# One-hots, gathers and turns in the expert stage of a gated cross-attention kernel

## The chip, the cores and the metric

The kernel runs on one core of one Trainium2 chip. The metric is the device time of one execution in microseconds (us). Before the change three runs took 1636.4, 1639.86 and 1645.21 us; the median, 1639.86, is the time before. A core has five engines, each with a queue of its own that it works off strictly in order: TensorE (PE in the profile; its weight loads are shown apart as PEld), VectorE (DVE), ScalarE (ACT), GpSimd (POOL) and SyncE (SP). [...]POOL, SP and ACT also issue transfers (DMAs).

## The reference

`x` is 4 batches of 512 rows of 512 numbers. Four residual blocks follow each other, each on a layer norm of `x`, each scaled by a gate:

```python
x = x + jnp.tanh(g_xattn[0]) * _L0_xattn_ref(_layernorm(x, axis=-1), fside_BxS2xS2_0, ctx_1024)
x = x + jnp.tanh(g_ffn[0]) * _L0_ffn_ref(_layernorm(x, axis=-1), L0_ffn_w_fc, L0_ffn_w_proj)
x = x + jnp.tanh(g_xattn[1]) * _L1_xattn_ref(_layernorm(x, axis=-1), ctx_1024, mask_BxS2_bf1, L1_xattn_Wq, L1_xattn_Wk, L1_xattn_Wv, L1_xattn_Wo)
x = x + jnp.tanh(g_ffn[1]) * _L1_ffn_ref(_layernorm(x, axis=-1), L1_ffn_router_w, L1_ffn_norm_w, L1_ffn_gate_w, L1_ffn_up_w, L1_ffn_down_w)
```

The first is a pair of 8-bit quantized linears, the second a ternary feed-forward, the third attention with 16 heads. The change concerns the fourth, a mixture of 8 experts of which each row uses the best 2:

```python
logits = router_in @ router_w.T
probs = jax.nn.softmax(logits, axis=-1)
topw, topi = jax.lax.top_k(probs, TOP_K)
topw = topw / jnp.sum(topw, axis=-1, keepdims=True)
cw = jnp.zeros((T, E), flat.dtype).at[jnp.arange(T)[:, None], topi].add(topw)
g = jnp.einsum('td,edf->tef', flat, gate_w)
u = jnp.einsum('td,edf->tef', flat, up_w)
a = jax.nn.silu(g) * u
expert_out = jnp.einsum('tef,efd->ted', a, down_w)
y = jnp.einsum('ted,te->td', expert_out, cw) * SCALE
```

## The kernel before

The kernel doesn't compute every expert for every row. It sorts the 2048 x 2 pairs of row and expert by expert into at most 39 tiles of 128 pairs (`NSEG`), each tile of one expert, and runs only these. Tiles 0 to 15 (`NA`) are full tiles found among the first three batches while the attention of the fourth is still running; tiles 16 to 38 (`NB`, 23 of them) hold the rest, and are found when the fourth batch has been routed.

Routing (`route`, from L709) normalizes a batch, scores the experts on TensorE, ranks them on VectorE and writes the rows, with their 8 weights behind the 512 numbers, to a table in memory (`xtab`). Sorting (`sort`, from L845) gives each pair a place, and then inverts the map from pair to place: with `hi` (the tile) and `lo` (the row in the tile) of each pair it builds one-hots, `in_row` (128 x 128 for each of 24 or 32 groups of rows, L907) and `in_seg` (two per group, as wide as there are tiles, L909; the second of the two is made by GpSimd), and sums their products on TensorE (L914) into the list of row numbers of each tile, `ids` (L925; `aids` for the first part, `bids` for the second). Both are generators: `step_beside` runs them a step at a time between pieces of other work, up to the next `yield`.

For each tile j the expert stage then does:

- `fetch`/`gather` (L985): an indirect DMA from POOL's queue brings the 128 rows, 520 wide, into one of eight buffers `xg`.
- turn: the rows must lie across the partitions for the matmuls. Either TensorE transposes them (`prepare`, `turn_by_tensor`, L1098, and VectorE copies the result, L1099), for the tiles in `by_tensor` (0 to 3, 16 to 19, 36 to 38); or VectorE transposes 32 x 32 blocks (`turn_rows`, L520) and, once four tiles are done, 16 transfers from SP set the blocks in place (L1089).
- `hide` (L1107) and `expert_in` (L1000): the gate and up products (L1005), silu on ACT (L1006), and on VectorE the product with the up half and the row's weight (L1007). `weight_of` (L992) picks that weight, `cwj`, from the gathered row by two small VectorE instructions (L996, L997), called from `hide`.
- `turn_hidden` (L1113): TensorE transposes the 128 x 256 result, VectorE copies it (L1099).
- `expert_out` (L1120): the down product (L1124), a copy on ACT to one of three buffers `y` (L1128), and an indirect scatter-add from POOL's queue onto the output (L1129). Each scatter waits for the one before to land, because two of them may add to the same row.

The loop at the end (from L1155) runs j from 0 to 39: fetch up to 9 tiles ahead, turn up to 6 ahead, `hide(j)`, `prepare(j + 1)`, `turn_hidden(j - 1)`, `expert_out(j - 2)`, two steps beside. The first two tiles are gathered and run in the last steps of the attention loop (`start_tile`, L1015), which is otherwise a steady round of four groups of matmuls a head (L599, L612, L637, L651) with their weights loaded from POOL's queue (L578 to L593).

The order in which an engine meets its instructions isn't that of the program. A scheduler reorders each engine's instructions before the kernel is built, by when it believes their inputs to be ready and by their place in the program. An instruction may so be set ahead of another that is needed sooner; on the chip, everything behind it waits.

## Time and profile before

The profiled execution took 1645.29 us; its span, from the first to the last instruction, is 1643.3 us.

| What | Value |
|---|---|
| TensorE busy in the span | 1522.8 us (93%) |
| VectorE, ScalarE, GpSimd busy | 926.9, 566.6, 465.8 us |
| mean granted TensorE clock | 0.972 |
| attention ends, expert stage begins | about 1380 us |
| TensorE busy from 1430 to 1640 us | 185.44 of 210 us, clock 0.96 |
| VectorE busy from 1430 to 1640 us | 63.74 of 210 us |
| scatter-adds (L1129): first and last start | 1401.1 and 1637.4 us |
| scatter-add, from issue to landing | median 4.8 us (2.7 to 6.3) |
| gather (L989), from issue to landing | median 3.9 us (3.3 to 7.3) |

In the timelines a row is: start in us, length in us, engine, line, operation, output and inputs, shapes, how many instructions were merged into the row, and in brackets how long the engine stood idle before it and what ended that wait. `x8` on a tile's matmuls means eight records for four products in 32-bit numbers. The chain of waits is followed back from the last instruction; its shares are of the whole span.

### The profile page before, as it was taken

To read this page: it belongs to the slowest core of one execution; us is meant where nothing else is said; L and a number is where in the kernel's file an instruction comes from. 1 tells how busy PE (TensorE), PEld (TensorE's weight loads), DVE (VectorE), ACT (ScalarE), POOL (GpSimd) and SP (SyncE) were. 2 spreads that over 40 slices of the span, in tenths; PEclk is the share of its full clock that TensorE was granted. 3 is DMA by queue.
4 is the path that set the end of the run, shared out by engine and by line. 5 is a ranking of instruction groups with operands and counts; after the bars stand their busy time and mean duration, and the time that the engine had idled before them with its cause. 6 is when DMAs were issued, how large, how long until landed. Compare 5 with 4: busy or idle time off the path is not lost. (4 is left out here: it accounts for less than half of the span.)

```text
span 1643.3 us, 16405 instructions
## 1 busy us (share of the span) xinstructions
PE 1522.8 (93%) x4404; PEld 785.6 (48%) x4412; DVE 926.9 (56%) x2422; ACT 566.6 (34%) x1180; POOL 465.8 (28%) x605
## 2 busy tenths in 40 slices
PE   4777888999999999999999999999999998978997
PEld 2434555676434444445444445444454444644563
DVE  5666777672155555585665765565758555734221
ACT  2645453633233333353333442333523322211111
POOL 1254324342211113131131131131314112454333
PEclk9997999999999999999999998999999999889999
DMA  8551200113445455575454574464754655457532
GB/s 299 200 191 66 65 20 33 31 67 90 134 137 151 139 140 154 141 208 156 106 160 136 155 195 117 133 184 134 200 158 134 159 144 151 105 104 154 103 64 28
DMA packets 115146, 215.59 MB, mean 131 GB/s; under 512 B 29984, under 2 KB 34080, under 8 KB 115056
## 3 DMA queue, kind: packets, MB, share of 16 engines
q1 hardware_dynamic: 72336, 103.89, 22.2%
q0 software_dynamic: 30896, 88.57, 21.6%
q10 hardware_dynamic: 11824, 22.09, 4.0%
q8 instruction: 37, 0.61, 0.2%
q14 instruction: 53, 0.43, 0.1%
HBM read 98.76 MB, written 35.72 MB: 82 GB/s over the span
## 5 line engine op out<-in xcount | busy, mean ns | idle before, releaser
L617 DVE CUSTOM_DVE_ANT_0 e<-bank,mask_b 128x512 f32<-128x512 f32 x256 | 175.1, 689 | 258.7 <-PE bank L612 258.5
L612 PE MATMUL bank<-kT,qT 128*128 128x512 f32 x512 | 232.3, 593 | 0.7 <-ACT dn L458 0.7
L651 PE MATMUL acc<-wo,oT 128*128 128x512 f32 x512 | 232.5, 596 | 0.3 <-ACT oT L641 0.3
L637 PE MATMUL bank<-eT,v 128*128 128x512 f32 x512 | 230.4, 592 | 1.8 <-DVE nmax L617 1.8
L620 ACT ACTIVATE e<-e,nmax 128x512 f32<-128x512 f32 x256 | 184.3, 720 | 97.5 <-DVE nmax L617 90.8
L599 PE MATMUL bank<-gu,wq 128*128 128x512 f32 x384 | 178.0, 601 | 2.3 <-DVE nmax L617 2.3
L514 DVE STREAM_TRANSPOSE blocks<-e 128x512 f32<-128x512 f32 x256 | 158.9, 678 | 22.6 <-DMA eT<-blocks 17.9
L637 PEld LDWEIGHTS bank<-eT,v 128*128 128x128 f32 x512 | 97.2, 190 | 124.6 <-issue 110.7
L651 PEld LDWEIGHTS acc<-wo,oT 128*128 128x128 f32 x512 | 97.7, 191 | 123.2 <-issue 120.3
L612 PEld LDWEIGHTS bank<-kT,qT 128*128 128x128 f32 x512 | 96.9, 190 | 124.7 <-issue 114.3
L641 ACT COPY oT<-bank 128x512 f32<-128x512 f32 x64 | 37.5, 585 | 300.4 <-PE bank L637 279.9
L578 POOL DMA_DIRECT2D wq<-in_L_xattn_Wq_dram x64 | 48.5, 758 | 265.3 <-PE bank L599 245.1
L599 PEld LDWEIGHTS bank<-gu,wq 128*128 128x128 f32 x384 | 73.2, 192 | 93.7 <-issue 82.2
L593 POOL DMA_DIRECT2D wo<-in_L_xattn_Wo_dram x64 | 36.9, 577 | 255.5 <-PE acc L651 250.4
L628 DVE TENSOR_SCALAR e<-e,rt 128x512 f32<-128x512 f32 x256 | 107.7, 484 | 2.1
L1005 PE MATMUL acc<-gu,turned 128*128 x224 | 102.9, 602 | 0.0
L603 ACT ACTIVATE qT<-bank 128x512 f32<-128x512 f32 x64 | 38.2, 597 | 170.2 <-PE bank L599 164.5
L405 PE MATMUL acc<-pjT,hT 128*128 128x512 f32 x320 | 87.5, 403 | 5.7 <-DVE hT L430 5.7
L418 PE MATMUL bank<-xfT,fcT 128*128 128x512 f32 x320 | 88.2, 407 | 0.0
L1005 PEld LDWEIGHTS acc<-gu,turned 128*128 128x128 f32 x224 | 65.9, 295 | 33.5 <-issue 8.2
L1124 PE MATMUL acc<-dn,hidT 128*128 x156 | 77.1, 619 | 0.6 <-DVE hidT L1099 0.6
L429 POOL TENSOR_TENSOR r<-r 128x512 f32<-128x512 f32 x40 | 42.2, 1058 | 95.5 <-ACT hT L428 95.5
(339 smaller groups left out, 2045.2 us busy)
## 6 DMA issues: line engine op xcount, KB each, us to landing
eT<-blocks SPq DMA_DIRECT2D x1016, 64.0 KB, 2.8
wq<-in_L_xattn_Wq_dram POOLq DMA_DIRECT2D x64, 256.0 KB, 3.9
wo<-in_L_xattn_Wo_dram POOLq DMA_DIRECT2D x64, 256.0 KB, 3.3
kd<-dn SPq DMA_DIRECT2D x32, 256.0 KB, 2.4
vd<-dn SPq DMA_DIRECT2D x32, 256.0 KB, 2.0
kT<-kd POOLq DMA_DIRECT2D x32, 256.0 KB, 3.9
v<-vd POOLq DMA_DIRECT2D x32, 256.0 KB, 4.0
turned<-blocks SPq DMA_DIRECT2D x112, 64.0 KB, 3.1
```

The lines of the kernel that those rows point to most:

```text
L405: nc.tensor.matmul(outs[t], lhsT=h[:, t * P : (t + 1) * P], rhs=pjT[:, j, :], start=(j == 0 and u == 0), stop=(j == NH - 1 and u == 1),)
L418: nc.tensor.matmul(ps, lhsT=fcT[:, i, j * P : (j + 1) * P], rhs=xT[u][:, i, :], start=(u == 0 and i == 0), stop=(u == 1 and i == KD - 1),)
L514: nc.vector.transpose(blocks[:, :, :, t, :].rearrange("p c s r -> p s c r"), src.rearrange("p (s c i) -> p s c i", c=NQ, i=Q))
L599: nc.tensor.matmul(ps, lhsT=th[:, i, :], rhs=xT[:, :, i, :], start=(i == 0), stop=(i == KD - 1))
L612: nc.tensor.matmul(ps, lhsT=qT[:, t * P : (t + 1) * P], rhs=kT, start=True, stop=True)
L617: nc.vector.tensor_tensor_reduce(e, ps, mask_b[b], -1.0, 3.0e38, ALU.add, ALU.min, nmax[:, t : t + 1])
L620: nc.scalar.activation(e, e, AF.Exp, bias=nmax[:, t : t + 1], scale=-1.0, accum_out=total[:, t : t + 1])
L628: nc.vector.tensor_scalar(es[:, t, :], es[:, t, :], rt[:, t : t + 1], None, ALU.mult)
L637: nc.tensor.matmul(ps, lhsT=v[:, s, :], rhs=eT[:, :, s, :], start=(s == 0), stop=(s == NT - 1))
L651: nc.tensor.matmul(sums[b][t], lhsT=oT[:, t * P : (t + 1) * P], rhs=to, start=(n == 0), stop=(n == NHEAD - 1))
L1005: nc.tensor.matmul(ps, lhsT=xgT[k], rhs=gu[:, bass.ds(e, 1), k, :], start=(k == 0), stop=(k == KD - 1))
L1124: nc.tensor.matmul(ps, lhsT=hT[f], rhs=dn[:, bass.ds(e, 1), f, :], start=(f == 0), stop=(f == NF - 1))
```

## The change

Six things change.

1. One-hots: the 24 or 32 small pairs of instructions become a few wide ones on VectorE, with broadcast operands. GpSimd makes none of them any more. There are fewer `yield`s, so the row numbers are traced a step or so earlier.
2. The first matmul over the one-hots, every gather, and every turn on VectorE are kept in program order: `tc.keep_in_program_order` sets an instruction behind the one traced before it on the same engine (an order only, no wait for it to finish). Others may still move around it.
3. The weight of a row is read where the tile is turned (`weigh_rows`), into a column of a small tile that lives for the whole stage, not where the product needs it. The buffer of gathered rows is free from then on.
4. Tiles 4 to 7 join the tiles turned by TensorE.
5. The copy of rows turned by TensorE (in `prepare`) goes from VectorE to ScalarE.
6. Leads: a tile turned by TensorE is fetched 4 steps ahead, one turned by VectorE 10 ahead and turned 7 ahead.

```diff
     def turn_tile_apart(src, blocks, t):
-        nc.vector.transpose(
+        return nc.vector.transpose(
...
+    tile_base = cp.tile([P, TT], F32, name="tile_base")
...
+        nc.vector.tensor_scalar(tile_base, col[:, :TT], float(P), None, ALU.mult)
...
-        for i in range(TOPK * nt):
-            s, t = divmod(i, nt)
-            nc.vector.tensor_scalar(in_row[:, i, :], col, lo[:, s, t : t + 1], None, ALU.is_equal)
-            for u, v in enumerate((row1[:, 0:1], float(P * t))):
-                (nc.gpsimd if u else nc.vector).tensor_scalar(in_seg[:, i, u, :], cols, hi[:, s, t : t + 1], v, ALU.is_equal, ALU.mult)
-            if i % 4 == 3:
+        m = TOPK * nt
+        at_tile = hi.rearrange("p s t -> p (s t)").unsqueeze(2).to_broadcast([P, m, n])
+        at_row = lo.rearrange("p s t -> p (s t)").unsqueeze(2).to_broadcast([P, m, P])
+        nc.vector.tensor_tensor(in_seg[:, :, 0, :], cols.unsqueeze(1).to_broadcast([P, m, n]), at_tile, ALU.is_equal)
+        for s in range(TOPK):
+            mine = slice(s * nt, (s + 1) * nt)
+            nc.vector.tensor_tensor(
+                in_seg[:, mine, 1, :],
+                in_seg[:, mine, 0, :],
+                tile_base[:, :nt].unsqueeze(2).to_broadcast([P, nt, n]),
+                ALU.mult,
+            )
+        nc.vector.tensor_scalar(in_seg[:, :, 0, :], in_seg[:, :, 0, :], row1[:, 0:1], None, ALU.mult)
+        yield
+        for i in range(0, m, 4):
+            nc.vector.tensor_tensor(
+                in_row[:, i : i + 4, :],
+                col.unsqueeze(1).to_broadcast([P, 4, P]),
+                at_row[:, i : i + 4, :],
+                ALU.is_equal,
+            )
+            if i % 8 == 4:
                 yield
+        yield
         ps = work_tile()
         for i in range(TOPK * nt):
-            nc.tensor.matmul(
+            mm = nc.tensor.matmul(
...
+            if i == 0:
+                tc.keep_in_program_order(mm)
...
-        nc.gpsimd.indirect_dma_start(xg, None, table, bass.IndirectOffsetOnAxis(ap=ids, axis=0))
+        tc.keep_in_program_order(
+            nc.gpsimd.indirect_dma_start(xg, None, table, bass.IndirectOffsetOnAxis(ap=ids, axis=0))
+        )
         return xg, owned

-    def weight_of(xg, owned):
-        cwj = small(1, "cwj")
+    row_weight = cp.tile([P, NSEG], F32, name="row_weight")
+    def weigh_rows(j, xg, owned):
         junk = small(NE, "junk")
         nc.vector.tensor_tensor(junk, xg[:, D:], owned, ALU.mult)
-        nc.vector.tensor_reduce(cwj, junk, AX.X, ALU.add)
-        return cwj
+        nc.vector.tensor_reduce(row_weight[:, j : j + 1], junk, AX.X, ALU.add)
...
-        nc.vector.scalar_tensor_tensor(h, h, cwj, ps[:, FE:], ALU.mult, ALU.mult)
+        nc.vector.scalar_tensor_tensor(h, h, row_weight[:, j : j + 1], ps[:, FE:], ALU.mult, ALU.mult)
...
-    by_tensor = {j for j in range(NSEG) if j < NT or j // NT == NA // NT or j >= NSEG - NSEG % NT}
+    by_tensor = {j for j in range(NSEG) if j < 2 * NT or j // NT == NA // NT or j >= NSEG - NSEG % NT}
...
-        turn_tile_apart(
-            got[j][0][:, :D], blocks_of[g].rearrange("p c (s t r) -> p c s t r", s=KD, t=NT), t
+        xg, owned = got.pop(j)
+        tc.keep_in_program_order(
+            turn_tile_apart(xg[:, :D], blocks_of[g].rearrange("p c (s t r) -> p c s t r", s=KD, t=NT), t)
         )
+        weigh_rows(j, xg, owned)
...
-    def turn_by_tensor(src, n, dst):
+    def turn_by_tensor(src, n, dst, copy=nc.vector.tensor_copy):
...
-            turned_in[j] = turn_by_tensor(got[j][0], KD, dst)
+            turned_in[j] = turn_by_tensor(got[j][0], KD, dst, nc.scalar.copy)
+            weigh_rows(j, *got.pop(j))
...
-    GATHER, TURN = 9, 6
-    next_fetch, next_turn = len(first), NT
+    lead = {j: 4 if j in by_tensor else 10 for j in range(len(first), NSEG)}
+    TURN = 7
+    to_fetch = sorted(lead, key=lambda j: (max(j - lead[j], 0), j))
+    to_turn = [j for j in to_fetch if j not in by_tensor]
     for j in range(NSEG + 1):
         known = NSEG if len(found) == NSEG else NA
-        while next_fetch < min(j + GATHER, known):
-            fetch(next_fetch)
-            next_fetch += 1
-        while next_turn < min(j + TURN + 1, next_fetch):
-            turn_rows(next_turn)
-            next_turn += 1
+        for t in [t for t in to_fetch if t - lead[t] <= j and t < known]:
+            fetch(t)
+            to_fetch.remove(t)
+        while to_turn and to_turn[0] - TURN <= j and to_turn[0] in got:
+            turn_rows(to_turn.pop(0))
```

More of the change, by code (lines that the diff above doesn't have):

```diff
@@ L988, in gather, with expert_in @@
         table = xtab[: TA * P, :] if j < NA else xtab[:, :]
-        nc.gpsimd.indirect_dma_start(xg, None, table, bass.IndirectOffsetOnAxis(ap=ids, axis=0))
+        tc.keep_in_program_order(
+            nc.gpsimd.indirect_dma_start(xg, None, table, bass.IndirectOffsetOnAxis(ap=ids, axis=0))
+        )
         return xg, owned
-    def weight_of(xg, owned):
-        cwj = small(1, "cwj")
+    row_weight = cp.tile([P, NSEG], F32, name="row_weight")
+    def weigh_rows(j, xg, owned):
         junk = small(NE, "junk")
         nc.vector.tensor_tensor(junk, xg[:, D:], owned, ALU.mult)
-        nc.vector.tensor_reduce(cwj, junk, AX.X, ALU.add)
-        return cwj
-    def expert_in(j, cwj, xgT, h):
+        nc.vector.tensor_reduce(row_weight[:, j : j + 1], junk, AX.X, ALU.add)
+    def expert_in(j, xgT, h):
         e = nc.tensor.value_load(found[j][1], min_val=0, max_val=NE - 1)
@@ L1021, in start_tile @@
         nc.vector.tensor_copy(xgT, tp)
-        first[j] = expert_in(j, weight_of(xg, owned), [xgT[:, k * P : (k + 1) * P] for k in range(KD)], first_hid[j])
+        weigh_rows(j, xg, owned)
+        first[j] = expert_in(j, [xgT[:, k * P : (k + 1) * P] for k in range(KD)], first_hid[j])
     for _ in queries_in(0):
@@ L1061 @@
     mo = ctx.enter_context(tc.tile_pool(name="moe", bufs=1, reuse_waits="tile"))
-    by_tensor = {j for j in range(NSEG) if j < NT or j // NT == NA // NT or j >= NSEG - NSEG % NT}
+    by_tensor = {j for j in range(NSEG) if j < 2 * NT or j // NT == NA // NT or j >= NSEG - NSEG % NT}
     blocks_of, turned_in, got = {}, {}, {}
     def fetch(j):
-        if j not in got:
-            got[j] = gather(j, mo.tile([P, ROW], F32, tag="xg", name="xg", bufs=8))
+        got[j] = gather(j, mo.tile([P, ROW], F32, tag="xg", name="xg", bufs=8))
     def turn_rows(j):
@@ L1080, in turn_rows @@
             blocks_of[g] = mo.tile([P, NQ, KD * P], F32, tag="blocks", name="blocks", bufs=2)
-        turn_tile_apart(
-            got[j][0][:, :D], blocks_of[g].rearrange("p c (s t r) -> p c s t r", s=KD, t=NT), t
+        xg, owned = got.pop(j)
+        tc.keep_in_program_order(
+            turn_tile_apart(xg[:, :D], blocks_of[g].rearrange("p c (s t r) -> p c s t r", s=KD, t=NT), t)
         )
+        weigh_rows(j, xg, owned)
         if t == NT - 1:
@@ L1098, in turn_by_tensor @@
             nc.tensor.transpose(tp[:, k * P : (k + 1) * P], src[:, k * P : (k + 1) * P], ident)
-        nc.vector.tensor_copy(dst, tp[:, : n * P])
+        copy(dst, tp[:, : n * P])
         return [dst[:, k * P : (k + 1) * P] for k in range(n)]
@@ L1110, in hide @@
             h = mo.tile([P, FE], F32, tag="hid", name="hid", bufs=3)
-            hidden[j] = expert_in(j, weight_of(*got.pop(j)), turned_in.pop(j), h)
+            hidden[j] = expert_in(j, turned_in.pop(j), h)
     def turn_hidden(j):
@@ L1178 @@
         step_beside()
-        if j == NA - GATHER // 2:
+        if j == NA - 4:
             while beside:
```

## The prediction

> **What bounds the kernel now.** I read the chain of waits first, since it tells what ended last. It holds 67 pieces from 1577 us to the end, and its head is one transfer repeated:

> ```profile
> DMA out_dram<-y,bids 3%; POOLq L1212 0%; POOLq L1129 0%
> ```

> Each expert tile ends in a scatter-add to the output (L1129), each of which waits for the one before it to land. I call them S0 to S38, and the gather of tile t's rows G(t). The timeline of POOL shows their pace at the end:

> ```profile
> 1615.35 1.55 POOL L1129 DMA_INDIRECT out_dram<-y,bids  x1 [4.07 <-DMA out_dram<-y,bids]
> 1620.88 1.55 POOL L1129 DMA_INDIRECT out_dram<-y,bids  x1 [3.98 <-DMA out_dram<-y,bids]
> 1626.55 1.55 POOL L1129 DMA_INDIRECT out_dram<-y,bids  x1 [4.12 <-ACT y L1128]
> 1637.40 1.55 POOL L1129 DMA_INDIRECT out_dram<-y,bids  x1 [1.92 <-DMA out_dram<-y,bids]
> ```

> The starts stand 5.5 us apart: from S16 (1521.71) to S35 (1626.55), 104.84 us in 19 steps, 5.52 each. The last three steps take 3.90, 3.48 and 3.47. TensorE's timeline has an expert tile every 5.37 us where it waits for nothing (tile starts 1594.99 and 1600.36). So two chains of nearly equal pace run side by side, and time lost by either before the tail is not won back. Hence I looked for lost time, first on POOL:

> ```profile
> 1425.91 1.55 POOL L1129 DMA_INDIRECT out_dram<-y,aids  x1 [8.19 <-ACT y L1128]
> 1426.92 15.68 POOL L909 TENSOR_SCALAR bin_seg<-col,bhi 128x23 bf16<-128x23 f32 x32
> 1442.87 1.60 POOL L1129 DMA_INDIRECT out_dram<-y,aids  x1 [0.27 <-issue]
> ...
> 1460.08 1.56 POOL L1129 DMA_INDIRECT out_dram<-y,aids  x1 [4.05 <-issue]
> 1461.94 1.04 POOL L989 DMA_INDIRECT xg<-xtab,bids  x1 [0.30 <-issue]
> ```

> S4's data was copied at 1430.42 (ACT's timeline), yet it started at 1442.87, because 32 small one-hot instructions held the queue. The first gather of the second part (G16), whose indices DVE had at 1448.25, stood behind four late scatters until 1461.94. VectorE and TensorE then stop:

> ```profile
> 1465.79 0.24 DVE L996 TENSOR_TENSOR junk<-xg,bowned 128x8 f32<-128x8 f32 x1 [17.53 <-DMA xg<-xtab,bids]
> 1466.80 0.69 PE L1098 MATMUL bank<-ident,hid 128*128 128x128 f32 x2 [10.55 <-DVE hid L1007]
> 1467.28 3.62 PE L1124 MATMUL acc<-dn,hidT 128*128 x4
> 1498.82 5.10 PE L1005 MATMUL acc<-gu,xgT 128*128 x8 [3.89 <-DVE xgT L1099]
> ```

> VectorE's queue holds the weight of a row tile just asked for ahead of the product that TensorE needs. The last two rows also ran at a low granted clock: 3.62 us against the usual 1.88, 5.10 against 3.60.

> **The change, part by part.** Times are in the profiled execution (span 1643.3; the run took 1645.29, the shown median is 1639.86). A difference found here is taken off both.

> *One-hots.* POOL loses L909: 10.82 us at 1235.58 and the 15.68 above. The first is worth nothing, since TensorE runs without a gap from 1216.94 to 1290. The second frees S4. VectorE had 64 small instructions in part two, spaced 0.20 us (12.9 us); it gets eight of 128x512 (nearest row L430, 714 ns), one compare of 736 elements, two products of 368 and one scaling of 736. L1007 takes 464 ns for 256, L430 714 for 512: 0.98 ns an element and 0.21 us. That gives 5.7 + 0.93 + 2 x 0.57 + 0.93 = 8.7 us (estimate; 6 if the scaling and products run at some faster rate, 13 if broadcasts cost half again). Cover: in the changed order the matmuls that read them (L914, 0.96 us, still there) stand after the output matmuls of tile 6, about 1441. VectorE starts near 1426 and has about 5 us of other work until then, so the cover holds to 10 us; without it TensorE and the next gather wait the 3 us that are over.

> [...]Row first: in 1410-1420 VectorE was busy 9.77 of 10 us, and the scatter at 1416.14 took 1.58 us to issue against 1.55 in the quiet tail. [...]

> *Gathers in program order.* In the changed order G20 follows S7, G21 S8, then two gathers follow each of S9 to S12 and one each of S13 to S22; G36 to G38 follow S29 to S31. A gather's 1.3 us on POOL fits under the 4 us that POOL waits for a scatter to land. With one in between, the steps S16 to S20 took 22.83 / 4 = 5.71, so I charge 5.71. Buffers: eight, released at the turn; by the two orders each is free before its gather's turn, but for G7, which waits for tile 4's transposes and holds S1 about 1 us, which S2 and S3, bound by their data, take back.

> What is late next is a gather. G16 and G22 follow S9 (new time about 1459.7), issue by 1464 and land 3.9 us later (median of the view of tile xg) at 1466-1467. The weights that read them stand on VectorE ahead of tile 12's transposed copy, due on TensorE about 1472. Five us are left; nothing is charged.

> *Weights at the turn.* The same 39 pairs (L996, L997, 0.32 us). The 17.53 stall goes: in the changed order no unlanded weight of the second part stands ahead of the products of tiles 9 to 11.

> *Turns.* Tiles 4 to 7 go to TensorE: 4 x 0.43 us (1609.17 to 1609.60 per tile) = +1.7 us of TensorE; VectorE loses 4 x 1.04 and SP 16 transfers. The copies move to ACT: 0.586 (L1128) against 0.684 on VectorE, in ACT's idle time. ACT now copies tiles 2 and 3 behind the store of the last block, issued at 1380.08: about +0.5 us to tile 2.

> *First gathers.* G0 and G1, issued at 1317.83 and 1332.62, now stand behind the weight load of 1348.73: issue near 1349.7 and 1351.0, landing 1354.9. VectorE's new order puts both weights ahead of tile 0's copy, so its matmuls start near 1355.7, not 1353.50: +2.2 us (from 0, if slack later takes it up, to 4). Ten weights now stand before tile 2's product (1392.70) and wait for gathers that land by about 1394: +1. Against these, the route of the last block has no turns in its way on VectorE (four, 3.8 us, stood at 1410-1414), and the 1.35 wait before L850 should mostly go. I take +1 us in all at S3 (bounds -3 and +5).

> **The sum, along the scatters.** S3 1425.9 + 1 = 1426.9. S4 5.6 later (the step from 1442.87 to 1448.48) 1432.5; S7 1449.3; fifteen steps with gathers at 5.71 to S22, 1535.0; S30 eight at 5.52, 1579.1; three at 5.71 to S33, 1596.2; two at 5.52 to S35, 1607.3; then 10.85 to S38, **1618.1**, against 1637.40: 19.3 us less. TensorE's own sum: from tile 7's start (1430.2, +1) its remaining work is 32 x 3.43 + 34 x 1.72 + 33 x 0.22 + 7 x 0.43 + 0.8 + 2 of tail waits = 181.4 us, ending 1612.6; S38 could start at 1614. So the scatters decide by 4 us. Span 1624, this execution's run 1626, median 1639.9 - 19 = **1621 us**.

> **Rivals.**

> 1. *The gathers slow the scatters.* From 1470.84 to 1521.71 the eight steps took 6.36 each, with up to two gathers between. If that is their price and not TensorE's stalls, 15 x 0.65 + 3 x 0.65 = 12 us come back: **1633**. Against it: steps of 5.7 with a gather later on. 15%.
> 2. *TensorE decides.* Scatters keep 5.4, or the start gains 3 us: S38 near 1612 and **1614**. For it: steps of 4.33 to 5.44 among 1555 to 1582. 22%.
> 3. *Slower: a ring.* A gather follows S(k), VectorE reads it ahead of hid and hidT, and these feed S(k+2): 1.9 + landing 3.9 + 0.3 + 0.9 + 0.2 + 1.9 + 0.7 = 9.8 us for two scatters, 4.9 each, under 5.5. It decides once the landing passes 5.3 us, and makes the kernel slower past about 7.6: nineteen gathers at 1.1 us cost 21. Landings of 7.3 did occur, beside the load of an expert's weights, none of which is left here. At 9.5 us of landing: 2.1 x 19 = 40, less 19: **1661**. 5%.
> 4. *The stalls move only.* Another queue head (ACT's copies, or the turns pinned on VectorE) stops TensorE as long as now: **1640**. For it: VectorE's pinned turns wait for a DMA with hid behind them. Against: 16 us between gather and turn. 8%.

> The forecast itself has 50%. Range: down to 1611 (rival 2 with 3 us more) and up to 1635 (rival 1 with the rule's 2.8). A measurement tells about 0.5%, 8 us, from no change. Rivals 1, 2 and the forecast lie beyond it but for a tail of rival 1: faster 0.85, same 0.09, slower 0.06.

> **What would show it.** No L909 on POOL; S4 5.6 us after S3; G20 right after S7; no TensorE wait over 3 us between 1400 and 1620; steps of 5.7 and 5.5; last scatter near 1618. A wait of POOL on xg buffers, of VectorE on xg transfers with TensorE behind it, or steps over 6 us would make me wrong.

## The result, and the profile after

Eight runs of each kernel were set beside each other: 1641.59 us before (median, 1636.4 to 1645.21), 1632.61 us after (1629.05 to 1636.03). The ratio is 0.9948, with a 95% interval of 0.9932 to 0.9964: a gain of 8.5 us (6 to 11) by the ratio, where 19 were forecast (1621 us). The direction is right and the time lies in the range, but the gain is less than half of what the sum says. Span of the profiled execution: 1631.1 us, granted clock 0.975.

Timeline of GpSimd after the change, the rows that answer to those shown of before (start, length, in brackets the idle time before and what ended it):

```profile
1432.63 1.57 POOL L1155 DMA_INDIRECT out_dram<-y,aids  x1 [8.17 <-ACT y L1154]
1438.44 1.56 POOL L1155 DMA_INDIRECT out_dram<-y,aids  x1 [4.24 <-ACT y L1154]
...
1455.60 1.55 POOL L1155 DMA_INDIRECT out_dram<-y,aids  x1 [4.40 <-ACT y L1154]
1457.45 1.02 POOL L1011 DMA_INDIRECT xg<-xtab,bids  x1 [0.30 <-issue]
1461.00 1.57 POOL L1155 DMA_INDIRECT out_dram<-y,aids  x1 [2.54 <-ACT y L1154]
...
1625.12 1.55 POOL L1155 DMA_INDIRECT out_dram<-y,bids  x1 [1.91 <-DMA out_dram<-y,bids]
```

The 15.68 us of one-hots between S3 and S4 are gone, S4 stands 5.8 us behind S3, and the first gather of the second part follows S7, as read from the order. All of this is close to the forecast. But S3 itself starts at 1432.63; it was forecast at 1426.9 and stood at 1425.91 before.

What comes before the expert stage isn't equally long in all executions: the last group of score products (L612) starts between 1336.8 and 1342.3 us in the fourteen profiles of this study. For a fair comparison I count from the start of that group, up to which the change was forecast to do nothing, and where the two stand a microsecond apart: 1341.41 before, 1340.42 after.

| from that start, us | before | forecast | after |
|---|---|---|---|
| S3 | 84.5 | +1 | 92.2 (+7.7) |
| S3 to S38 | 211.5 | 191.2 | 192.5 |
| S38 | 296.0 | -19.3 | 284.7 (-11.3) |

**From S3 on the total came out within 1.3 us of the sum. The miss is the start**, which the forecast put at "+1 us in all": of the 8.0 us by which this pair of profiles falls short of 19.3, 6.7 lie ahead of S3. (The other 2.8 us, from the 11.3 of this pair to the 8.5 of the medians, may be scatter of single executions: the profiled one of before took 1645.29 us, 3.7 more than its median, and that of after 1632.85, close to its own.)

TensorE's timeline at the start, after:

```profile
1347.29 3.60 PE L637 MATMUL bank<-eT,v 128*128 128x512 f32 x8
1353.69 0.97 PE L1042 MATMUL bank<-ident,xg 128*128 128x128 f32 x4 [2.80 <-DMA xg<-xtab,aids]
1356.51 4.87 PE L1028 MATMUL bank<-gu,xgT 128*128 x6 [1.86 <-DVE row_weight L1021]
...
1388.19 8.68 PE L1028 MATMUL acc<-gu,xgT 128*128 x16 [2.57 <-DVE row_weight L1021]
...
1424.99 0.23 PE L852 MATMUL bank<-sel,earlier 128*128 128x128 bf16 x1 [2.62 <-DVE sel L780]
1425.58 0.27 PE L855 MATMUL bank<-past,ones_b 128*128 128x128 bf16 x1 [0.35 <-DVE past L782]
1425.68 2.07 PE L1028 MATMUL acc<-gu,xgT 128*128 x2
1427.54 0.21 PE L809 MATMUL bank<-past,ones_b 128*128 128x8 bf16 x1
1427.61 1.75 PE L1028 MATMUL acc<-gu,xgT 128*128 x2
```

The same places before:

```profile
1351.71 0.60 PE L1019 MATMUL bank<-ident,xg 128*128 128x128 f32 x4
1353.50 3.70 PE L1005 MATMUL bank<-gu,xgT 128*128 x8 [1.19 <-DVE xgT L1021]
...
1418.27 0.22 PE L850 MATMUL bank<-sel,earlier 128*128 128x128 bf16 x1 [1.35 <-DVE sel L778]
```

There are three things to see. Tile 0 waits for its gather, a wait that did not exist before. The wait for `sel` (the marks of the experts that each row uses, the end of the router's ranking), which "should mostly go", has grown from 1.35 to 2.62. And what follows a wait is slow: two records of products take 2.07 and 1.75 us where they take 1.08 and 1.07 elsewhere. VectorE's timeline says why `sel` is late:

```profile
1414.90 0.19 DVE L763 TENSOR_TENSOR pr<-pr,r_mx 128x32 f32<-128x32 f32 x1
1420.01 0.24 DVE L1020 TENSOR_TENSOR junk<-xg,aowned 128x8 f32<-128x8 f32 x2 [4.92 <-DMA xg<-xtab,aids]
1420.21 0.24 DVE L1021 TENSOR_REDUCE row_weight<-junk 128x1 f32<-128x8 f32 x2
1420.36 0.17 DVE L765 TENSOR_REDUCE r_mx<-pr 128x4 f32<-128x32 f32 x1
```

The router's ranking (`r_mx`) stands in VectorE's queue behind the weight of a tile whose gather is still under way. It is the fault of the kernel before (17.53 us before L996), smaller and at another place. The gather in question was issued at 1415.82, in order behind S1 (1413.93), and landed at 1419.98; before, all sixteen gathers of the first part had been issued by 1400.83. So two parts of the change meet here: a gather kept in order, and a weight that is free to move ahead of the ranking.

The windows of TensorE give what the rows hint at. Columns: stretch, its length, TensorE's busy time (records), granted clock (1.00 is full speed), busy share of the DMA engines, GB/s that they moved.

```profile
1350.90:1353.90 3.00, 0.21 (x2) 0.99 0.87 250
1353.90:1360.30 6.40, 4.54 (x9) 0.50 0.62 144
1386.00:1388.00 2.00, 0.00 (x0) 0.99 0.91 230
1388.00:1391.40 3.40, 3.21 (x4) 0.50 1.04 361
...
1422.40:1425.20 2.80, 0.21 (x1) 1.00 0.57 64
1425.20:1428.40 3.20, 2.85 (x6) 0.55 0.60 135
```

After each of these waits TensorE works at about half clock for 3.2 to 6.4 us. What it loses by that while it is busy, no bracket shows.

So I read two losses from windows of half a microsecond, from L612's start to the end of S3's own products (2.6 us ahead of S3): idle time, and busy time times (1 - granted clock). S3 less both stood at 69.0 us before, 68.9 after, and between 67.8 and 70.6 in all kernels of this study, where S3 itself goes from 79.0 to 92.2. So these two numbers are most of what moves S3. From before to after idle grew by 4.9 (7.6 to 12.5), the loss to the clock by 2.8 (8.0 to 10.8): together the 7.7 us.

### The profile page after: what moved, and what is told of

It is laid out like the page before. It is cut to its first block, busy times and chain, and to the rows that moved or that the text cites. A ratio compares the mean times of both kernels' runs of the same rounds, so it can differ in the third digit from the quotient of the medians.

```text
span 1631.1 us, 16266 instructions
## 1 busy us (share of the span) xinstructions
PE 1523.0 (93%) x4420; PEld 785.1 (48%) x4428; DVE 905.7 (56%) x2320; ACT 574.3 (35%) x1193; POOL 442.4 (27%) x549
## 5 line engine op out<-in xcount | busy, mean ns | idle before, releaser
L612 PE MATMUL bank<-kT,qT 128*128 128x512 f32 x512 | 232.3, 594 | 0.7 <-ACT dn L458 0.7
L612 PEld LDWEIGHTS bank<-kT,qT 128*128 128x128 f32 x512 | 97.1, 190 | 124.6 <-issue 115.3
L1028 PE MATMUL acc<-gu,turned 128*128 x192 | 86.5, 594 | 0.0
L1028 PEld LDWEIGHTS acc<-gu,turned 128*128 128x128 f32 x192 | 56.5, 295 | 27.9 <-issue 5.5
L405 PEld LDWEIGHTS acc<-pjT,hT 128*128 128x128 f32 x320 | 59.6, 189 | 19.4 <-DVE hT L430 7.3
```

What stands on the lines that cost most here:

```text
L405: nc.tensor.matmul(outs[t], lhsT=h[:, t * P : (t + 1) * P], rhs=pjT[:, j, :], start=(j == 0 and u == 0), stop=(j == NH - 1 and u == 1),)
L612: nc.tensor.matmul(ps, lhsT=qT[:, t * P : (t + 1) * P], rhs=kT, start=True, stop=True)
L1028: nc.tensor.matmul(ps, lhsT=xgT[k], rhs=gu[:, bass.ds(e, 1), k, :], start=(k == 0), stop=(k == KD - 1))
```

## The experiments

**Theory**: two parts of the change that were priced at little make the start late: the first two gathers kept in program order, and weights hoisted ahead of the layer norm and the router on VectorE. **Rivals**: four more tiles on TensorE and their copies on ScalarE; or the time is set after S3, whatever the start does.

### Taking the two back, one by one and together

`e_first`, in `gather`:

```diff
-        tc.keep_in_program_order(
-            nc.gpsimd.indirect_dma_start(xg, None, table, bass.IndirectOffsetOnAxis(ap=ids, axis=0))
-        )
+        asked = nc.gpsimd.indirect_dma_start(xg, None, table, bass.IndirectOffsetOnAxis(ap=ids, axis=0))
+        if j >= len(first_hid):
+            tc.keep_in_program_order(asked)
```

`e_wpin`, in `weigh_rows`; `e_first_wpin` has both edits:

```diff
-        nc.vector.tensor_tensor(junk, xg[:, D:], owned, ALU.mult)
+        tc.keep_in_program_order(nc.vector.tensor_tensor(junk, xg[:, D:], owned, ALU.mult))
```

> The kernel after, but the gathers of tiles 0 and 1 are not kept in program order (all others are). Theory 'start': the pin on these two is the larger part of what the start lost. TensorE then waits for no transfer before tile 0 (after: 2.80 us), tile 0's products start 3 to 4 us earlier against the end of the attention, and S3 starts near 1429 instead of 1432.6; all later steps keep their length, so the run is 3 to 4 us shorter than after (ratio to before about 0.992 to 0.993). Rival 'four more tiles': the start is late because of tiles 4 to 7 on TensorE and their copies on ScalarE; then tile 0 comes earlier, but S3 moves by less than 1.5 us and the ratio stays at 0.994 to 0.995. Rival 'elsewhere': the time is set after S3 in any case, and a shift of S3 is taken up later: S3 earlier, last scatter within 1 us of after.

> The kernel after, but the first of the two instructions that read a row tile's weight is kept in program order on VectorE, so that it can't be set ahead of the layer norm's and the router's chain. Theory 'start': VectorE's waits of 4.92 us ahead of the ranking and some 5 us ahead of the layer norm go, TensorE's wait of 2.62 us for sel goes or falls below 1 us, S3 is 2 to 3 us earlier than after (1429.6 to 1430.6), and the run is as much shorter (ratio about 0.993). Rival 'four more tiles': sel is late because the router itself starts 3.7 us later, the weights only fill a wait that is there anyway: S3 within 1 us of after, ratio 0.994 to 0.996. Rival 'new queue head': pinned weights hold products in the later stage, steps over 6 us, ratio above 0.996.

> Both edits of the two runs beside it. Theory 'start': the two add up; S3 near 1426 to 1428 (forecast: 1426.9), 5 to 6.5 us shorter than after, 1626 to 1628 us, ratio 0.990 to 0.9915. If they overlap (the router waits for the same gathers either way), the better of the two alone: 0.992 to 0.993. Rival 'four more tiles': 0.994 to 0.995.

| | ratio to before (interval) | S3 | S3 to S38 | idle | lost to clock |
|---|---|---|---|---|---|
| before | 1 | 84.5 | 211.5 | 7.6 | 8.0 |
| after | 0.9948 (0.9932 to 0.9964) | 92.2 | 192.5 | 12.5 | 10.8 |
| `e_first` | 0.9921 (0.9899 to 0.9944) | 88.9 | 192.4 | 9.9 | 10.2 |
| `e_wpin` | 0.9885 (0.9864 to 0.9907) | 87.5 | 189.2 | 9.3 | 9.6 |
| `e_first_wpin` | 0.9863 (0.9839 to 0.9888) | 80.2 | 189.4 | 5.9 | 5.1 |

(S3, idle and clock in us, counted as above, in one profiled execution each. The runs came from several chips, so ratios are compared here and below, each against runs of before on the same chip.) The theory holds. The rival of four more tiles is out, since these are in all three; the rival after S3 is out, since S3 to S38 doesn't grow when S3 comes earlier (192.4, 189.2, 189.4 against 192.5). I had expected the weights to bring 2 to 3 us and both edits 5 to 6.5; by the ratios they brought about 10 and 14 of 1641, so I underrated them a second time. Two parts of that can be seen. Ahead of S3 `e_wpin` has 3.2 us less idle time and 1.2 less lost to the clock. And the weights also bring some 3 us behind S3, which I had not reckoned with: with either form of the first gathers S3 to S38 falls (192.5 to 189.2, 192.4 to 189.4), about half of it in the last three steps (12.3 to 10.8). By the ratios the two edits simply add up (about 4 and 10 against 14). In the profiles both together take 12.0 us off S3, against 3.3 and 4.7 alone, but these are single executions (that of `e_wpin` was the slowest of its five), and the order of TensorE differs too: in `e_first` it stands idle for 2.34 us ahead of tile 0's products, with half clock behind (0.50 for 3.4 us from 1352.5), because VectorE copies the turned rows late; in `e_first_wpin` it comes to these rows later and stands for 0.83. `e_first_wpin`, in the rows where after had its worst:

```profile
1416.18 0.22 PE L852 MATMUL bank<-sel,earlier 128*128 128x128 bf16 x1
1416.23 1.08 PE L1028 MATMUL acc<-gu,xgT 128*128 x2
1417.15 0.17 PE L809 MATMUL bank<-past,ones_b 128*128 128x8 bf16 x1
1417.18 0.22 PE L855 MATMUL bank<-past,ones_b 128*128 128x128 bf16 x1
1417.23 1.07 PE L1028 MATMUL acc<-gu,xgT 128*128 x2
```

There is no bracket ahead of `sel`, and the products behind it take their usual time. This kernel, at 1618.5 us, is faster than before and after.

### The price of the first gathers, by itself

`b_firstpin`: the kernel before, with only G0 and G1 kept in program order.

```diff
-        nc.gpsimd.indirect_dma_start(xg, None, table, bass.IndirectOffsetOnAxis(ap=ids, axis=0))
+        asked = nc.gpsimd.indirect_dma_start(xg, None, table, bass.IndirectOffsetOnAxis(ap=ids, axis=0))
+        if j < len(first_hid):
+            tc.keep_in_program_order(asked)
```

> The kernel before with one edit: the gathers of tiles 0 and 1 are kept in program order, as in the kernel after. Theory 'wait and clock': TensorE waits 2.5 to 3 us for the first gather and then runs at half clock for 3.4 or 6.8 us: S0 4 to 6 us later against the end of the attention, all of it kept: ratio 1.0025 to 1.0035. Theory 'forecast' (2.2 us, the wait alone): 1.0013. Rival 'absorbed': the later stalls take it up, 0.9995 to 1.0005.

Measured: 1.0035 (1.0024 to 1.0045), 5.7 us slower, against a price of 2.2 in the forecast. Its TensorE:

```profile
1351.44 1.09 PE L1021 MATMUL bank<-ident,xg 128*128 128x128 f32 x4 [2.94 <-DMA xg<-xtab,aids]
1353.63 5.13 PE L1007 MATMUL bank<-gu,xgT 128*128 x6 [1.09 <-DVE xgT L1023]
```

The wait is 2.94, and the products run at 0.50 for 6.8 us. So the forecast's price, the wait alone, is too low, and "wait and clock" is what the run bears out. In this one profile S3 is 3.8 us later than before, less than the 5.7 of the medians: idle time grew by 3.0 us, but the spells of half clock at later places happened to be shorter, so that the loss to the clock as a whole did not grow (7.9 against 8.0).

### Which weights

`fw_turned`: as `e_first_wpin`, but weights of the tiles turned by TensorE (that is, 0 to 7 at the start) may move.

```diff
-        nc.vector.tensor_tensor(junk, xg[:, D:], owned, ALU.mult)
+        read = nc.vector.tensor_tensor(junk, xg[:, D:], owned, ALU.mult)
+        if j not in by_tensor:
+            tc.keep_in_program_order(read)
```

> The kernel with the first gathers free, and of the weights only those of tiles turned by VectorE (8 to 15, 20 to 35) are kept in order, behind their turn; those of tiles 2 to 7 may be set ahead. Theory 'start, by the turned tiles': the harm came from weights of tiles 8 and later, which stood ahead of the layer norm's and the router's chain while their gathers had just been asked for; with these in order alone the kernel is as fast as with all weights in order: no wait of TensorE for sel, S2 to S3 6 us (11 in after), ratio 0.985 to 0.988. Rival 'any weight': those of tiles 2 to 7 do the harm, TensorE's wait for sel stays at 2.3 us with half clock behind it, and the ratio stays at that of the first gathers alone, 0.991 to 0.993.

Measured: 0.9881 (0.9856 to 0.9905), at the slow edge of the first expectation; the interval overlaps that of `e_first_wpin`, so only the profiles tell the two apart. At the start it is as that theory says: `sel` isn't waited for, S3 at 79.0. What it lost (S3 to S38 takes 195.8 us, against 189.4) comes with a wait of 4.89 us at a place I had not thought of. VectorE and TensorE at 1573:

```profile
1572.81 0.17 DVE L1020 TENSOR_TENSOR junk<-xg,bowned 128x8 f32<-128x8 f32 x1 [13.62 <-DMA xg<-xtab,bids]
1572.89 0.42 DVE L1127 COPY hidT<-bank 128x256 f32<-128x256 f32 x1
1573.23 0.47 DVE L1032 SCALAR_TENSOR_TENSOR hid<-hid,row_weight,acc 128x256 f32<-128x256 f32 x1
```

```profile
1573.76 0.69 PE L1126 MATMUL bank<-ident,hid 128*128 128x128 f32 x2 [4.89 <-DVE hid L1032]
```

A weight still left free (only those of tiles 16 to 19 and 36 to 38 were, by then) moved up the queue and held `hidT` and `hid`, as in the kernel before. So the harm at the start comes from tiles 8 and later, and a weight left free did the same elsewhere.

### Wait or clock

`fw_warm`: `e_first_wpin` with 16 transposes that nobody reads, set in the wait ahead of tile 2's products (for this tile 3's own transposes are traced ahead of them); `fw_t4_warm` the same with tiles 4 to 7 on VectorE.

```diff
+        for _ in range(16 if j == 2 else 0):
+            nc.tensor.transpose(ps[:, :P], rows_of_3[0][:, :P], ident)
         for k in range(KD):
```

> The kernel with both edits (first gathers free, weights in order; 1618.5), and 16 extra transposes on TensorE (of rows of tile 3, into the bank that tile 2's products then overwrite) in the 2.69 us in which it waits for the copy of tile 2's rows. Nothing starts earlier by them; only TensorE has no gap there. Theory 'wait and clock': the 3.3 us at half clock that follow the gap (1383.8 to 1387) are gone, tile 2's and 3's products take 7.1 instead of 8.80 us, 1.6 us shorter in this place; 1616 to 1618 in all, ratio 0.985 to 0.986. Rival 'wait alone': the granted clock falls there as before, or the products take as long; 1618 to 1620.

> The same extra transposes in the kernel with both edits and with tiles 4 to 7 turned by VectorE (1617.6). Theory 'wait and clock': 1.6 us shorter, 1615 to 1617, ratio about 0.984. Rival 'wait alone': 1617 to 1619.

First the two rows of `e_first_wpin`, the gap and what follows; then the same place in `fw_warm`, and its next gap:

```profile
1380.50:1383.70 3.20, 0.51 (x1) 0.98 0.90 247
1383.70:1387.00 3.30, 3.30 (x5) 0.50 1.01 350
```

```profile
1380.30:1382.10 1.80, 1.80 (x19) 1.00 0.75 139
1382.10:1389.00 6.90, 6.90 (x19) 1.00 0.97 356
1390.50:1393.20 2.70, 0.62 (x4) 0.98 0.94 301
1393.20:1396.60 3.40, 3.38 (x8) 0.52 0.02 5
```

With the gap filled the clock stays at 1.00, and the products of tiles 2 and 3 take 7.03 instead of 8.80 us: the slowness is the gap's doing, not the products'. The time in all is 0.9852 (0.9835 to 0.9869), not to be told from 0.9863. In the profile the gain was taken up at once: TensorE came earlier to the layer norm's transposes, waited 1.62 us there for ScalarE, and got its spell of half clock there. `fw_t4_warm` gave 0.9873 (0.9854 to 0.9891), no gain either over its base, `fw_t4`, below. So the mechanism is shown, and filling this one gap brings nothing that these runs can tell from zero.

### What the one-hots bring

`b_onehot`: the kernel before with the wide one-hots alone (and the first of the matmuls over them in order, as in the change). `fw_narrow`: `e_first_wpin` with the old ones, so that these 32 instructions stand on GpSimd again:

```diff
-        nc.vector.tensor_tensor(in_seg[:, :, 0, :], cols.unsqueeze(1).to_broadcast([P, m, n]), at_tile, ALU.is_equal)
...
+            for u, v in enumerate((row1[:, 0:1], float(P * t))):
+                (nc.gpsimd if u else nc.vector).tensor_scalar(in_seg[:, i, u, :], cols, hi[:, s, t : t + 1], v, ALU.is_equal, ALU.mult)
```

> The kernel before with the wide one-hots on VectorE alone: gathers, turns, weights and leads stay as they were. Theory 'forecast': S4 follows S3 after about 5.6 us instead of 17, the first gather of the second part starts near 1452 instead of 1461.94 (it still stands behind S6), TensorE's stall of 10.55 us shrinks to between 1 and 4 us; S3 stays at 1425.9 since the start is untouched. Steps after that 5.5 to 5.7: 8 to 10 us shorter than before, ratio 0.994 to 0.995, as much as the whole change. Rival 'order of the gathers': weights that wait for gathers hold VectorE as long as before, and the stall only moves: 0.998 to 1.000. Rival 'cover': VectorE's 7 to 8 us of wide instructions hold hid or hidT and TensorE waits for them, 1.000 or more.

> The kernel with both edits, but with the one-hots as they were before the change: small instructions, half of them on GpSimd (15.7 us in the second part). Theory 'forecast': S4 waits for them again, 10 to 11 us late, and of this 8 to 11 us stay: 1627 to 1630, ratio 0.991 to 0.993. Rival 'order of the gathers does it': with gathers and weights in order TensorE has work in hand, and the scatters, which can be 5 us apart where TensorE takes 5.4, win it back: under 4 us stay, 1618.5 to 1622, ratio 0.986 to 0.9885.

`b_onehot`: 0.9956 (0.9942 to 0.9971), 7.2 us: a little under what I expected, and not to be told from the whole change. TensorE's longest wait after S3 is 3.83 (10.55 before). `fw_narrow`: 0.9920 (0.9901 to 0.9939), 9 us more than `e_first_wpin`, as the forecast's theory says; S4 starts 16.9 us after S3. So the one-hots are worth 7 us in the old order and 9 in the new. S3 to S38 takes 211.5 us before, 201.0 with the one-hots alone and 192.5 after: the other parts of the change bring another 8.5 there, and S3 comes 7.7 later than before. That is why the whole looks like the one-hots alone.

One row of `b_onehot` has a bearing on a term of the sum. GpSimd, then VectorE:

```profile
1427.74 4.39 POOL L1150 DMA_INDIRECT out_dram<-y,aids  x1 [3.84 <-ACT y L1149]
```

```profile
1427.02 3.69 DVE L922 TENSOR_TENSOR in_row<-col,blo 128x512 bf16<-128x512 f32 x6
```

This scatter took 4.39 us to issue, 2.8 more than the usual 1.55. It began while VectorE made six one-hots in a row, and ended 1.4 us after the last of them. It isn't an accident of this run. Of the eleven kernels with wide one-hots, ten have one such scatter, of 1.77 to 4.39 us, and each of them began while a wide TENSOR_TENSOR of the one-hots was running on VectorE (in the eleventh, `fw_warm`, that one ended 0.1 us after the scatter began); no other scatter in any of the fourteen kernels took over 1.7. Where the scatter began first and the wide one came behind, it took 1.55 or 1.56 us.

### The other parts

Each as `e_first_wpin` with one edit: `fw_t4`: tiles 4 to 7 turned by VectorE again; `fw_cdve`: the copies in `prepare` on VectorE again; `fw_free`: no gather kept in order.

```diff
-    by_tensor = {j for j in range(NSEG) if j < 2 * NT or
+    by_tensor = {j for j in range(NSEG) if j < NT or
```
```diff
-            turned_in[j] = turn_by_tensor(got[j][0], KD, dst, nc.scalar.copy)
+            turned_in[j] = turn_by_tensor(got[j][0], KD, dst)
```
```diff
-        if j >= len(first_hid):
-            tc.keep_in_program_order(asked)
```

> The kernel with both edits (first gathers free, weights in order), but tiles 4 to 7 are turned by VectorE again. Theory 'forecast': four tiles less for TensorE, 4 x 0.43 = 1.7 us: 1 to 2 us shorter than with both edits (1618.5), ratio near 0.9855. Rival 'turns in the way': the four turns, kept in order on VectorE, stand ahead of the layer norm's chain and wait for their gathers; xnl and sel come 3 to 5 us later, with a spell of half clock after each wait: 1621 to 1625, ratio 0.988 to 0.990.

> The kernel with both edits, but the copies of the rows that TensorE turned are made by VectorE again instead of ScalarE. Theory 'forecast' (ScalarE's copies cost 0.5 us before tile 2 and nothing later): 0 to 1 us shorter, 1617.5 to 1618.5, ratio 0.986. Rival 'VectorE's queue': two copies ahead of the layer norm's chain and two in the router's chain make sel late by 1.5 to 3 us: 1620 to 1622, ratio 0.987 to 0.9885.

> The kernel with both edits, but no gather at all is kept in program order; the leads stay. Seven gathers of the second part then stand in one row between two scatters. Theory 'order matters': 7 x 1.3 = 9 us of GpSimd between S7 and S8 or so, 3.5 us more than a step, and gathers that wait there for buffers hold the scatters longer: 3 to 8 us longer than with both edits, 1621 to 1627, ratio 0.988 to 0.992. Rival 'TensorE decides': scatters catch up since TensorE's chain is the longer one: within 1 us of 1618.5, ratio 0.986.

| | ratio (interval) | S3 | S3 to S38 |
|---|---|---|---|
| `fw_t4` | 0.9849 (0.9828 to 0.9870) | 81.9 | 189.8 |
| `fw_cdve` | 0.9887 (0.9867 to 0.9908) | 79.1 | 196.8 |
| `fw_free` | 0.9883 (0.9864 to 0.9902) | 81.7 | 193.4 |

`fw_t4` can't be told from `e_first_wpin` (0.9863): the turns that I feared ahead of the layer norm cost S3 1.7 us in one profile, and the medians show nothing of it. The rival (0.988 to 0.990) is out; the 1.7 us that the forecast's theory would save are too few to be seen. `fw_cdve` was slower, near what its rival said, but not for its reason: `sel` was not late; TensorE waited 3.60 us for `hid` at 1427, where VectorE's queue then held `in_row`, turns and copies, and the next products ran at half clock (5.37 instead of 3.60). So the move of the copies to ScalarE seems to earn about 4 us in this order, but the two intervals overlap. `fw_free` came out slower as 'order matters' said, at the lower end, with overlapping intervals too: seven gathers stood in a row, and S7 started 10.7 us after S6.

## Why the prediction was right and wrong

**One-hots**: right. The GpSimd block of 15.68 us and the stall of 10.55 went, and nothing took their place after S3 (TensorE's longest wait there is 1.18). VectorE's wide ones took 7.4 us (0.90 + 0.97 + 0.42 + 5.10 for the eight) against 8.7 forecast.

**Wide instructions and GpSimd**: the top of the range (1635) holds 2.8 us for scatters held up by wide instructions on VectorE, a term that no run shows. The one row of before that the forecast sets beside it, a scatter that took 1.58 us to issue against 1.55, stood beside shorter instructions (of 0.21 to 0.47 us each) and proves nothing for these. What the runs showed in its place: in after, S5 took 1.95 us to issue beside two one-hots, 0.4 lost; in `b_onehot`, a scatter beside six without a break took 4.39, 2.8 lost. So there is a delay beside wide instructions here; what makes it, no trace shows. That the change escapes most of it because turns and `hid` stand between its one-hots fits these rows, but was not tested.

**Gathers in order**: right in place and price. S3 to S22 took 107.8 us against 108.1, S22 to S30 44.9 against 44.1. Rival 1 (they slow the scatters) and rival 3 (a ring) are out. But the chain that decides was taken wrongly: of the 36 scatters from S3 on, 24 show a copy of `y` as what released them last, and 8 the scatter before, so TensorE set the pace after S3. That the sum survived is luck: the two chains lay very near each other. It is rival 2's mechanism, with a time of 1632.6 and not 1614, since TensorE started late and its sum was too low: from tile 7's start (1437.38) S38 came 187.7 us later, where the sum has 182.8.

**The tail**: 12.3 us from S35 to S38 against 10.85. TensorE waited 0.99 and 0.61 us for the last `hid` and `hidT`.

**The start, the step that failed**: "+1 us in all at S3 (bounds -3 and +5)". Measured +7.7, outside the bounds. Its terms:

- "First gathers: +2.2". The issue times were read rightly (G0 at 1348.61, G1 at 1349.96), and TensorE's added waits, 2.80 and 0.67, make 3.5, inside the 0 to 4. What isn't in the term is the half clock behind them (6.4 us at 0.50 here). The order of these two gathers by itself cost 5.7 (`b_firstpin`).
- "Ten weights ... +1" and "the 1.35 wait before L850 should mostly go". The weights were looked for only ahead of tile 2's product. In the layer norm's way VectorE waited 4.9 us for gathers in three steps (1.45, 2.67, 0.79), and in the router's way another 4.92; the wait for `sel` grew instead of going. Put in order on VectorE (`e_wpin`), they were worth about 10 us, some 3 of them behind S3.
- No term for the clock. The forecast had quoted two rows "at a low granted clock" behind the old stall, and then priced every new wait by its length alone. What such a term needs, the profiles show from 1340 us on: behind a stretch of 3.41 us with at most 1.64 us of work in it the granted clock fell to 0.50, 43 times with one exception, and the spells between L612 and S3 that follow a wait last 3.4 or 6.8 us (last section). In after they are 6.83, 3.41 and 3.41 us, behind stretches with 0.61, 0.66 and 0.50 us of work. Priced so, each of three new or longer waits would have carried another 0 to 3.4 us (an estimate: half of a spell of 0 to 6.8 us).

The sign set down for this ("no TensorE wait over 3 us between 1400 and 1620") came true and still let the miss through: the longest wait, 2.62, is under 3, and the rest lies before 1400. Another sign did warn: "VectorE on xg transfers with TensorE behind it" is just what the 4.92 and the 2.62 are. And two steps passed 6 us (6.09 and 6.42), with no harm to the total.

**Rival 4** (the stalls only move) named the right mechanism, another queue head, but the wrong one (copies, turns) and the wrong place. It came true in part.

What stays open: the medians differ by 2.8 us less than the two profiles. The granted clock differs between executions of one kernel (0.969 to 0.975 in the eleven runs of before set beside `fw_t4_warm`), so the spells of half clock may be the reason; each kernel has one profile, so this isn't shown. Nor is it shown how the 4.92 us of the router's wait divide between the gather that came late and the weight that came early: no run frees the one and leaves the other.

## What to carry to other kernels

When an instruction that waits for a transfer is traced earlier or kept in order, read in the new order what stands behind it on its engine at every place where it can land, the start of the stage above all, and tie it to its place if a scheduler can hoist it. Price a wait of TensorE as its length plus half of the spell at half clock that may follow; in these profiles, between L612 and S3, such a spell lasted 0, 3.4 or 6.8 us, which makes 0, 1.7 or 3.4 us, by where the wait falls. And fix the reference point ahead of the change: a sum along a chain is only as good as the time at which the chain starts.

## What was not expected of the hardware

The same gap doesn't always cost the same. Ahead of the products of tiles 2 and 3 TensorE idles 2.35 to 2.70 us in nearly every kernel of this study. These are the products in before, `e_first_wpin` and `fw_turned`:

```profile
1383.04 10.11 PE L1005 MATMUL acc<-gu,xgT 128*128 x16 [2.35 <-DVE xgT L1099]
```

```profile
1383.19 8.80 PE L1028 MATMUL acc<-gu,xgT 128*128 x16 [2.69 <-issue]
```

```profile
1381.59 7.10 PE L1030 MATMUL acc<-gu,xgT 128*128 x16 [2.70 <-ACT ln_y L150]
```

After nearly the same gap the spell lasts 6.8 us, 3.4 us or not at all. The granted clock tells why. In each of the fourteen profiles, from 1340 us on, the spells start whole multiples of 3.41 us apart and last 3.4, 6.8 or 10.2 us (only those that run into the end of the kernel differ). In after they start at 1353.83, 1387.97, 1405.03 and 1425.51, which is 0, 10, 15 and 21 times 3.41 us behind the first. So the time can be cut into stretches of 3.41 us, counted from any start of a spell. These are such stretches in the three kernels above, in the same order:

```profile
1378.82:1382.24 3.42, 1.21 (x9) 1.00 0.68 166
1382.24:1385.65 3.41, 2.61 (x3) 0.50 1.03 398
1385.65:1389.06 3.41, 3.41 (x5) 0.50 0.98 354
```

```profile
1380.14:1383.56 3.42, 0.73 (x5) 1.00 0.89 248
1383.56:1386.97 3.41, 3.41 (x5) 0.50 1.02 355
```

```profile
1376.54:1379.95 3.41, 1.71 (x10) 1.00 0.79 172
1379.95:1383.37 3.42, 1.78 (x4) 1.00 0.95 360
```

One place doesn't fit. The clock falls without a gap too: 2.5 to 5.6 us into the router's narrow products (L752 in after, 128x8, 6.89 us) it is halved for 6.8 or 10.2 us in every kernel profiled here, behind a stretch in which TensorE was busy throughout; the window from 1405.00 to 1415.20 of after has 10.20 us busy at 0.50. Why is not shown.
